# A two-layer graph network on one core: gathers behind one wait, look-ahead maxima from two tiles, sums copied a window later

## The chip, the cores and the metric

The kernel runs on 1 core of one Trainium2 chip. The metric is device time in microseconds (us) for one execution. The kernel before took 2846.57 us (median of 3 runs, 2844.92 to 2849.02).

## What is computed

The graph has N = 6250 nodes with 512 features (8 heads of 64) and E = 100000 edges, sorted by destination. Two layers follow each other, each with a normalisation in front and a residual behind:

```python
h = relu(layernorm(x))
# layer 0: attention over incoming edges
h = leaky_relu(h @ W.T + b)                       # 6250 x 512
e = leaky_relu(e_src[src] + e_dst[dst])           # per edge and head
m = segment_max(e, dst);  ex = exp(e - m[dst]);  s = segment_sum(ex, dst)
x = x + segment_sum(h[src] * (ex / s[dst] * dist), dst)
# layer 1: mean over incoming edges
h = relu(layernorm(x))
neigh = segment_sum(h[src], dst) / max(deg, 1)
y = h @ W_self.T + neigh @ W_neigh.T + bias
x = x + layernorm(y) * gamma + beta
```

## The kernel before

**Prologue** (up to about 320 us). The product `h @ W.T + b` goes to DRAM as rows of 520 values (512 features and 8 source logits), and index tables are built.

**Windows.** The edge list is cut into four streams (`NQ = 4`) that are walked side by side. A window is three tiles (`T = 3`) of 128 edges from each stream, 12 tiles in all, and there are 66 windows (`NW`; the last has one tile per stream). Streams 0 and 1 form pair p = 0, streams 2 and 3 pair p = 1. A tile is named (q, j): stream q, tile j of the window.

**Layer 0, edges** (about 320 to 1540 us). For each tile GpSimd gathers 128 rows of `h` by an indirect DMA (L719; 12 per window, in the order of `tiles`, stream by stream) into one of `NB = 4` buffers, so that `gather(k + 4)` at the end of the loop's round k refills the buffer that window k has just left. TensorE builds the one-hot of the destinations' transpose (`front_turn`, L781), multiplies it with the destinations' logits (`front_dst`, FD, L793), and adds the source logits (`soft_src`, SS, L799), which ScalarE has picked out of the gathered rows (`soft_pick`, EC, L805). So EC waits until all 12 gathers of its window have landed. VectorE finds the running maxima by three scans: `max_ahead` (NX, L824) over the next window's first two tiles backwards (`LA = 2`), `max_before` (SCF, L817) and `max_all` (SCR, L831). Two transposes (TE, TM, L843), a copy (CM), and LM, SUB, EXP, AA give the edges' weights. The weights are multiplied into the gathered rows: `message` on VectorE for tiles j = 0 and 1 (D0a, D0b, D1a, D1b, L937), and 28 pieces per window on ScalarE for most of tile 2 (H01 to H13, L956). TensorE sums the rows by destination: `add_up` (A00 to A12, L969 and L972; Apj is pair p, tile j), with `finish` (C0, C1, L980 and L981) to carry sums over from the window before. The sums of a pair fill one PSUM bank and are copied out by EV0 and EV1 (L990, L992) and stored to DRAM by `store` (L1003, SyncE's queue). A matrix product of 32-bit floats appears as two records per matmul, so an add_up is 4 records on L969 and 4 on L972.

**The order** of all this is written by hand. `ORDER` is a list of step names, gone through once per round k; `STEPS` says which window (k plus an offset) a name works on; every engine executes its own instructions in that order. "S" and "L" advance the node work (layer 0's normalisation, `slot_run`) that is mixed in.

**Layer 1, edges** (about 1590 to 2760 us). Here `gather1` (L1238) brings the 12 tiles of a window into a pool of five half-window buffers, `add_up1` (L1267) sums them, `finish1` adds the carry (L1274, two matmuls from the parts `chi` and `clo`) and copies the sums out of PSUM at once (L1277), `carry_split` (L1288, L1289) splits them for the next window's carry. Between these steps the loop at L1509 advances `slot1_run`, the dense part for 128 nodes: transposes (`turned`, L1334) with the copies `hi` and `lo` right behind them (L1335, L1336), 24 matmuls (L573), statistics and output.

Of the kernel before, what the change touches and what calls it, by code (L numbers as in the profile page):

```python
# [19 lines left out]
NQ = 4  # L20
NL = 196
ES = NL * 128
T = 3
# [21 lines left out]
def gnn_kernel(ctx, tc, x, srcp, dstp, attrp, wt0, b0, wsrc, wdst, wts, wtn, bias1, gamma1, beta1, out):  # L45
# [666 lines left out]
    def gather(k):  # L712
        GT[k] = g_ = gbuf[:, k % NB]
        tiles = [(q, j) for q in range(NQ) for j in range(njof(k))]
        if k >= NW - 3:
            tiles.sort(key=lambda t: t[1])
        for q, j in tiles:
            c = k * T + j
            G.indirect_dma_start(out=g_[:, q, j, :], out_offset=None, in_=h0_d,  # L719
                                 in_offset=bass.IndirectOffsetOnAxis(ap=idx[:, q, c:c + 1], axis=0))  # L720
# [73 lines left out]

    def soft_src(k):

        z, es = ZP[k], ES_.pop(k)
        for j in range(njof(k)):
            P.matmul(z[0:NQ * H, j * 128:j * 128 + 128], es[:, j], ident, start=False, stop=True,  # L799
                     skip_group_check=True)  # L800

    def soft_pick(k):
        nj = njof(k)
        ES_[k] = es = lp.tile([128, T, NQ * H], FT, name="es")
        A.activation(es[:, 0:nj].rearrange("p j (q h) -> p j q h", q=NQ),  # L805
                     GT[k][:, :, 0:nj, D:RW].rearrange("p q j h -> p j q h"), AF.Copy)

# [283 lines left out]
    def slot(w):  # L1091
# [140 lines left out]
    def gather1(k):  # L1232
        for p in range(2):
            GT[k, p] = g_ = g1.tile([128, 2, T, D], FT, name="g")
            for q2 in range(2):
                for j in range(njof(k)):
                    c = k * T + j
                    G.indirect_dma_start(out=g_[:, q2, j, :], out_offset=None, in_=h1_d[0:NT * 128, :],  # L1238
                                         in_offset=bass.IndirectOffsetOnAxis(ap=idx[:, 2 * p + q2, c:c + 1], axis=0))
# [19 lines left out]
    HL = {}  # L1259

    def add_up1(k, p, j):
        if j >= njof(k):
            return
        if j == 0:
            BK[p] = bank("w", 2)
        for q2 in range(2):
            P.matmul(BK[p][64 * q2:64 * q2 + 64, :], OHs[k][:, p, j, q2], GT[k, p][:, q2, j, :], start=(j == 0),  # L1267
                     stop=False, skip_group_check=True)

    def finish1(k, p):  # L1270
        w = BK.pop(p)
        if k:
            for part in HL.pop((k - 1, p)):
                P.matmul(w, CS[k][:, p], part, start=False, stop=True, skip_group_check=True)  # L1274
        if p == 0:
            WS[k] = lp.tile([128, 2, D], FT, name="ws")
        A.activation(WS[k][:, p], w, AF.Copy)  # L1277
        GT.pop((k, p))
        if p:
            OHs.pop(k)  # L1280
            CS.pop(k, None)
            WS.pop(k - 2, None)

# [30 lines left out]
    def own_run(s):  # L1314
        r, hs = SA.pop(s)
        hi, lo = parts_of(0)
        turned(hs, "t", hi, lo)
        yield
        pm = bank("m", 2)
        product(pm, hi, lo, wsh, wsl, [False])  # L1320
        P.matmul(pm, ones2, rows1, start=False, stop=True)
        yield
        OWN[s] = own = own_place(s)
# [5 lines left out]

    def turned(src, tag, hi, lo):  # L1330

        pt = bank(tag)
        for k in range(4):
            P.transpose(pt[:, k * 128:k * 128 + 128], src[:, k * 128:k * 128 + 128], ident)  # L1334
        A.activation(hi.rearrange("p k n -> p (k n)"), pt, AF.Copy)  # L1335
        V.tensor_tensor(out=lo.rearrange("p k n -> p (k n)"), in0=pt, in1=hi.rearrange("p k n -> p (k n)").bitcast(FT),  # L1336
# [25 lines left out]
    def slot1_run(s):  # L1362
        r, hs, sx, sa = SA.pop(s)
        parts = []
        for i, (src, tag) in enumerate(((hs, "t"), (sa, "z"))):
            if src is not None:
                parts.append(parts_of(i))
                turned(src, tag, *parts[-1])
            yield
        pm = bank("m", 2)  # L1370
        last = [False]
# [135 lines left out]

    last = none()
    for k in range(-1, NW - 1):  # L1509
        if k + 1 in own_at:  # L1510
            own_load(own_at[k + 1])
        early(k - 1, slot1_sums)
# [6 lines left out]
        when(k, add_up1, 0, 1)  # L1519
        step(last)  # L1520
        step(sl_)
        when(k, add_up1, 0, 2)
        step(last)
        when(k, finish1, 0)
        when(k, store, 0, acc1_d, D)
        step(last)
        step(last)
        step(sl_)
        when(k, add_up1, 1, 0)
        step(last)  # L1530
        when(k, carry_split, 0)
        step(last)
        when(k, add_up1, 1, 1)
        step(last)
        step(last)
        when(k + 1, onehot, 3)
        step(last)
        when(k, add_up1, 1, 2)
        step(last)
        when(k, finish1, 1)  # L1540
        when(k, store, 1, acc1_d, D)
        when(k, carry_split, 1)
        when(k + 1, carry_sel, FR)
        run(last)
        put_out()
        if k < NW - 2:
            step(sl_)
        early(k - 1, slot1_mean)
        run(pre)
        last = sl_  # L1550
        if k >= 0:
            when(k + 3, gather1)
    k = NW - 1
    early(k - 1, slot1_sums)
    sl_ = early(k - 2, slot1_run)
    for p in range(2):
        for j in range(T):
            add_up1(k, p, j)
        finish1(k, p)
        store(k, p, acc1_d, D)  # L1560
    for i in range(NLATE):
        late_sums(i)
    step(last)
    step(sl_)
    step(sl_)
    step(last)
    step(sl_)
# [166 lines left out]
```

## Time and profile before

| quantity | value |
|---|---|
| median of 3 runs | 2846.57 us |
| the profiled execution's own time | 2820.21 us |
| its span, first to last instruction | 2818.4 us |
| TensorE busy (PE) | 2164.9 us, 77% |
| GpSimd busy (POOL) | 1702.9 us, 60% |
| VectorE busy (DVE) | 1601.4 us, 57% |
| ScalarE busy (ACT) | 1115.8 us, 40% |
| layer 0 gathers, L719 | 784, mean 964 ns |
| layer 1 gathers, L1238 | 784, mean 982 ns |
| gathers' queue (q0), share of 16 DMA engines | 50.1% |
| mean granted TensorE clock | 0.868 |

The profiled execution ran 26 us below the median of the timed ones. Busy shares are means over stages with different limits, so a stage is read from a stretch of its own. In the timeline an entry gives the start, the length, the engine, the line, the operation, and in brackets how long the engine had been idle and what ended that; "issue" is a wait that the profile can't tell, "remote" a release without a sender in the profile.

### The profile page before, as it was taken

What the parts mean: (1) busy time and instruction counts of PE and PEld (TensorE: products, weight loads), DVE (VectorE), ACT (ScalarE), POOL (GpSimd) and SP (SyncE); (2) the same over time, 40 slices, a digit from 0 to 9 for tenths busy, and PEclk for the clock granted to TensorE, in tenths of its full rate; (3) what the DMA queues carried; (4) which work ended last, traced back from release to release, by engine and by line L of the source; (5) the groups of instructions that cost most, each with busy time, mean ns of one, the idle gap of its engine ahead of it and who ended that gap; (6) DMA issues with size and microseconds to landing.
All of it is one profiled execution on the core that took longest, in us unless ns stands there. A gap on an engine that the chain in (4) does not pass through costs nothing.

```text
span 2818.4 us, 35919 instructions
## 1 busy us (share of the span) xinstructions
PE 2164.9 (77%) x9688; PEld 1096.7 (39%) x9688; DVE 1601.4 (57%) x3323; ACT 1115.8 (40%) x3374; POOL 1702.9 (60%) x1679
## 2 busy tenths in 40 slices
PE   7993587878778778777787157797888888788775
PEld 5761244334333334333333023343433434343343
DVE  8875366566666566666667312254545445454556
ACT  5750355555555556555555201122222222222222
POOL 4665456556555556556562556666666666666662
PEclk9996688888888888889889578898999899899988
DMA  6535567777777777777776667777887787787862
GB/s 210 187 114 148 142 188 192 202 227 225 225 233 224 218 236 231 228 221 232 226 225 179 211 185 212 239 248 252 247 257 251 253 254 243 253 251 254 255 218 87
DMA packets 264720, 611.74 MB, mean 217 GB/s; under 512 B 63605, under 2 KB 74373, under 8 KB 264511
## 3 DMA queue, kind: packets, MB, share of 16 engines
q0 software_dynamic: 125440, 414.35, 50.1%
q1 hardware_dynamic: 138494, 193.97, 21.1%
q8 instruction: 80, 1.31, 0.2%
q14 instruction: 130, 1.06, 0.1%
q10 hardware_dynamic: 576, 1.05, 0.1%
HBM read 511.44 MB, written 97.76 MB: 216 GB/s over the span
## 4 chain that ended last, share of the span: by engine, by line
PE 33%; issue 21%; DVE 17%; another core or an unknown queue 11%; ACT 10%; DMA 3%; SPq 3%; POOL 1%; ACTq 0%; DVEq 0%; POOLq 0%
PE ps_w L969 9%; PE ps_w L1267 6%; ACT gbuf L956 4%; PE ps_f L573 3%; PE ps_b L573 3%; PE ps_w L980 2%; PE ps_w L1274 2%; DVE gbuf L937 2%; SPq L1003 1%; DVE hr L613 1%; POOL gbuf L719 1%; DVE clo L1289 1%; PE ps_z L793 1%; PE ps_w L573 1%
## 5 line engine op out<-in xcount | busy, mean ns | idle before, releaser
L719 POOL DMA_INDIRECT gbuf<-h_d,idx x784 | 756.1, 964 | 511.3 <-issue 251.5
L1238 POOL DMA_INDIRECT g<-h_d,idx x784 | 769.5, 982 | 395.0 <-issue 217.9
L969 PE MATMUL ps_w<-gbuf,oh 128*64 128x512 f32 x1568 | 533.0, 724 | 84.1 <-issue 62.0
L1267 PE MATMUL ps_w<-g,oh 128*64 128x512 f32 x1568 | 432.2, 652 | 104.2 <-issue 80.6
L956 ACT ACTIVATE gbuf<-gbuf,aa 128x64 f32<-128x64 f32 x1788 | 457.5, 336 | 11.2 <-DVE aa L877 5.7
L937 DVE TENSOR_TENSOR gbuf<-gbuf,ps_c 128x1024 f32<-128x1024 f32 x260 | 305.1, 1200 | 0.0
L1277 ACT ACTIVATE ws<-ps_w 128x512 f32<-128x512 f32 x132 | 78.8, 597 | 473.4 <-remote 144.6
L1288 DVE CAST chi<-ws 128x512 fp32r<-128x512 f32 x130 | 57.5, 442 | 354.0 <-issue 253.3
L1267 PEld LDWEIGHTS ps_w<-g,oh 128*64 128x64 f32 x1568 | 100.2, 146 | 275.7 <-issue 243.3
L990 ACT ACTIVATE ws<-ps_w 128x512 f32<-128x512 f32 x132 | 78.3, 593 | 260.7 <-remote 120.6
L817 DVE TENSOR_TENSOR_SCAN mf<-penb,mf,ps_z 32x384 f32<-32x384 f32 (+1 forms) x65 | 64.5, 992 | 204.6 <-ACT e L811 104.5
L608 POOL TENSOR_TENSOR pr<-hr,watt 128x1024 f32<-128x1024 f32 x47 | 113.2, 2410 | 91.3 <-DVE hr L606 75.6
L969 PEld LDWEIGHTS ps_w<-gbuf,oh 128*64 128x64 f32 x1568 | 106.9, 155 | 142.3 <-issue 106.0
L762 DVE TENSOR_TENSOR oh<-ps_c,dsr 128x768 f32<-128x768 f32 x130 | 123.4, 950 | 55.3 <-remote 26.7
L972 PEld LDWEIGHTS ps_s<-ex,oh 128*64 128x64 f32 x792 | 79.2, 161 | 181.8 <-issue 181.5
L972 PEld LDWEIGHTS ps_f<-ex,oh 128*64 128x64 f32 x776 | 73.1, 160 | 191.4 <-issue 190.5
L980 PE MATMUL ps_w<-ws,cs 128*128 128x512 f32 x228 | 138.2, 690 | 0.0
L573 PE MATMUL ps_f<-ws_whi,hi 128*128 128x512 f32 x112 | 55.6, 497 | 90.3 <-ACT hi L1335 52.2
L781 PE MATMUL ps_t<-ident,oh 128*128 128x128 f32 x392 | 75.5, 304 | 55.1 <-issue 22.2
L793 PE MATMUL ps_z<-oht,edb 128*32 128x384 f32 (+1 forms) x264 | 101.5, 509 | 19.5 <-issue 19.1
L824 DVE TENSOR_TENSOR_SCAN nx<-penb,ms,ps_z 32x256 f32<-32x256 f32 x66 | 47.5, 720 | 115.2 <-remote 94.2
L1336 DVE TENSOR_TENSOR lo<-ps_t,hi 128x512 fp32r<-128x512 f32 x55 | 37.9, 689 | 112.3 <-ACT hi L1335 67.2
(388 smaller groups left out, 3932.7 us busy)
## 6 DMA issues: line engine op xcount, KB each, us to landing
sx<-x SPq DMA_DIRECT2D x95, 256.0 KB
acc_d<-ws SPq DMA_DIRECT2D x182, 130.2 KB
acc_d<-ws SPq DMA_DIRECT2D x182, 128.0 KB
h_d<-hr SPq DMA_DIRECT2D x49, 260.0 KB
gbuf<-h_d,idx POOLq DMA_INDIRECT x784
g<-h_d,idx POOLq DMA_INDIRECT x784
sa<-acc_d SPq DMA_DIRECT2D x48, 260.5 KB
s<-acc_d SPq DMA_DIRECT2D x48, 256.0 KB
```

The source lines that it names most:

```text
L573: P.matmul(pt, a_[:, k], w_[:, k], start=not last[0], stop=stop and k == 3 and w_ is whi_ and a_ is lo)
L608: (G if t < NT - 2 else V).tensor_tensor(out=pr, in0=hr[:, None, 0:D].to_broadcast([128, 2, D]), in1=watt, op=OP.mult)
L719: G.indirect_dma_start(out=g_[:, q, j, :], out_offset=None, in_=h0_d, in_offset=bass.IndirectOffsetOnAxis(ap=idx[:, q, c:c + 1], axis=0))
L762: V.tensor_tensor(out=oh.rearrange("p a j b n -> p (a j b) n"), in0=c_iota[:, None, :].to_broadcast([128, 4 * T, M]), in1=dsr[:, k].rearra ...
L793: P.matmul(z[0:NQ * H, 0:n], ed_tile(k, p), oht[:, p, 0:n], start=(p == 0), stop=False, skip_group_check=True)
L937: eng.tensor_tensor(out=x4, in0=x4, in1=(AA if eng is V else A2)[k][:, i, q].unsqueeze(3).to_broadcast([128, 2, H, D // H]), op=OP.mult)
L956: A.activation(x_, x_, AF.Copy, scale=A2[k][:, T - 1, 2 * p + q2, h:h + 1])
L969: P.matmul(w[r, :], oh[:, p, j, q2], g_[:, 2 * p + q2, j, 0:D], start=(j == 0), stop=False, skip_group_check=True)
L972: P.matmul(sv[r, p], oh[:, p, j, q2], ex[:, j, 2 * p + q2], start=(j == 0 and p == 0), stop=False, skip_group_check=True)
L980: P.matmul(w, CS[k][:, p], c[:, p, 0:D], start=False, stop=True, skip_group_check=True)
L1238: G.indirect_dma_start(out=g_[:, q2, j, :], out_offset=None, in_=h1_d[0:NT * 128, :], in_offset=bass.IndirectOffsetOnAxis(ap=idx[:, 2 * p ...
L1267: P.matmul(BK[p][64 * q2:64 * q2 + 64, :], OHs[k][:, p, j, q2], GT[k, p][:, q2, j, :], start=(j == 0), stop=False, skip_group_check=True)
```

## The change

In layer 0:

- `gather` issues tile (3, 2) first, then the tiles j = 0, j = 1 and j = 2 of all streams (before: stream by stream). The last three windows keep their order. Tile (3, 2) is the one whose buffer is read last, by A12.
- EC and SS are split. ECa and SSa do tiles 0 and 1, at the end of the round before the one in which EC and SS stood; ECb and SSb do tile 2.
- `load_edges` loads pair 1 before pair 0.
- `ORDER` is new.

In layer 1:

- `gather1` goes tile by tile (before: stream by stream).
- `finish1` no longer copies the sums. `evac1_` does, in the next window, and issues the stores. The sums use three PSUM banks in turn instead of two.
- `turned` is split into `turn_on` (transposes) and `halves` (`hi`, `lo`), with other steps between them; the dense part of a slot ends one window later, and the loop's order is new.

```diff
     def gather(k):
...
-        if k >= NW - 3:
-            tiles.sort(key=lambda t: t[1])
+        tiles.sort(key=lambda t: (t != (NQ - 1, T - 1) or k >= NW - 3, t[1]))
...
     def load_edges(k):
...
-        for p in range(2):
+        for p in (1, 0):
...
+    def parts(k, i):
+
+        return range(0, min(LA, njof(k))) if i == 0 else range(LA, njof(k))
+
+    def soft_src(k, i):
+
+        for j in parts(k, i):
+            P.matmul(ZP[k][0:NQ * H, j * 128:j * 128 + 128], ES_[k, i][:, j - i * LA], ident, start=False, stop=True,
                      skip_group_check=True)
+        ES_.pop((k, i), None)
+
+    def soft_pick(k, i):
+        js = parts(k, i)
+        if js:
+            ES_[k, i] = es = lp.tile([128, (LA, T - LA)[i], NQ * H], FT, name=f"es{i}")
...
-        FD=(3, front_dst), EC=(2, soft_pick), SS=(2, soft_src), EZ=(2, soft_copy), SCF=(2, max_before), NX=(2, max_ahead),
+        FD=(3, front_dst), ECa=(3, soft_pick, 0), SSa=(3, soft_src, 0), ECb=(2, soft_pick, 1), SSb=(2, soft_src, 1), EZ=(2, soft_copy), SCF=(2, max_before), NX=(2, max_ahead),
...
-    H01 S CS H10 FT1 D0a S TE EC SS A00 D1a H11 D0b S H02 EV1 RESC H03 D0c L S A01 AT0 OH S A10 FT1c H12 D1b A02 S NX S SCR RS
-    FL FDf FX RH S C0 AT0c FT0 AT1 H13 EV0 S A11 TM EZ SCF S CM LM PF S SUB F9a F9b S A12 EXP S C1 AA AT1c FD S FT0c
+    FT1 S H10 D0a TE S H01 L CS D1a A00 D0b ECb NX SCR EV1 RESC A01 H13 D0c A10 S H03 SSb S H02 S FT1c H12 OH H11 AT0 S
+    TM FL FDf FX CM D1b A02 LM S RS SUB EZ S RH C0 FT0 AT0c EV0 AT1 SCF S EXP PF S A11 AA S F9a A12 F9b C1 AT1c FD ECa
+    S SSa S FT0c
...
     def gather1(k):
...
-            for q2 in range(2):
-                for j in range(njof(k)):
+            for j in range(njof(k)):
+                for q2 in range(2):
...
+    def bank_s():
+
+        s_[0] = (s_[0] + 1) % 3
+        return bank("s") if s_[0] == 0 else bank("w", 2)
...
     def finish1(k, p):
...
-        if p == 0:
-            WS[k] = lp.tile([128, 2, D], FT, name="ws")
-        A.activation(WS[k][:, p], w, AF.Copy)
+        BK[k, p] = w
...
+    def evac1_(k, p):
+        if p == 0:
+            WS[k] = lp.tile([128, 2, D], FT, name="ws")
+        A.activation(WS[k][:, p], BK.pop((k, p)), AF.Copy)
+        store(k, p, acc1_d, D)
...
     def slot1_run(s):
...
+                pts.append(turn_on(src, tag))
             yield
+        for i, pt in enumerate(pts):
+            parts.append(parts_of(i))
+            halves(pt, *parts[-1])
+        yield
...
-    last = none()
+    last, ends = none(), none()
     for k in range(-1, NW - 1):
...
+        when(k - 1, evac1_, 0)
+        early(k - 2, slot1_mean)
+        step(sl_)
         when(k, add_up1, 0, 0)
+        step(ends)
+        when(k - 1, carry_split, 0)
...
+        when(k, finish1, 0)
         step(sl_)
+        run(ends)
+        put_out()
+        when(k - 1, evac1_, 1)
+        early(k - 1, slot1_sums)
+        when(k, add_up1, 1, 0)
+        when(k - 1, carry_split, 1)
...
-        last = sl_
+        last, ends = sl_, last
```

More of the change, by code (lines that the diff above doesn't have):

```diff
@@ L793, in front_dst @@
             P.matmul(z[0:NQ * H, 0:n], ed_tile(k, p), oht[:, p, 0:n], start=(p == 0), stop=False, skip_group_check=True)
-    def soft_src(k):
-        z, es = ZP[k], ES_.pop(k)
-        for j in range(njof(k)):
-            P.matmul(z[0:NQ * H, j * 128:j * 128 + 128], es[:, j], ident, start=False, stop=True,
-                     skip_group_check=True)
[L802 to L806, printed above, removed]
+    def parts(k, i):
[3 more added lines that the diff above has]
+            P.matmul(ZP[k][0:NQ * H, j * 128:j * 128 + 128], ES_[k, i][:, j - i * LA], ident, start=False, stop=True,
+                     skip_group_check=True)
+        ES_.pop((k, i), None)
[3 more added lines that the diff above has]
+            ES_[k, i] = es = lp.tile([128, (LA, T - LA)[i], NQ * H], FT, name=f"es{i}")
+            A.activation(es[:, 0:len(js)].rearrange("p j (q h) -> p j q h", q=NQ),
+                         GT[k][:, :, js[0]:js[-1] + 1, D:RW].rearrange("p q j h -> p j q h"), AF.Copy)
     def soft_copy(k):
@@ L1234, in gather1 @@
             GT[k, p] = g_ = g1.tile([128, 2, T, D], FT, name="g")
-            for q2 in range(2):
-                for j in range(njof(k)):
+            for j in range(njof(k)):
+                for q2 in range(2):
                     c = k * T + j
@@ L1259, in gnn_kernel @@
     HL = {}
+    s_ = [0]
+    def bank_s():
+        s_[0] = (s_[0] + 1) % 3
+        return bank("s") if s_[0] == 0 else bank("w", 2)
     def add_up1(k, p, j):
@@ L1264, in add_up1 @@
         if j == 0:
-            BK[p] = bank("w", 2)
+            BK[p] = bank_s()
         for q2 in range(2):
@@ L1281, in finish1 @@
             CS.pop(k, None)
+    def evac1_(k, p):
[3 more added lines that the diff above has]
+        store(k, p, acc1_d, D)
+        if p:
             WS.pop(k - 2, None)
@@ L1315, in own_run @@
         r, hs = SA.pop(s)
+        pt = turn_on(hs, "t")
+        yield
+        yield
         hi, lo = parts_of(0)
-        turned(hs, "t", hi, lo)
+        halves(pt, hi, lo)
         yield
@@ L1321, in own_run @@
         P.matmul(pm, ones2, rows1, start=False, stop=True)
+        yield
         yield
@@ L1328, in parts_of, with turn_on @@
         return [lp.tile([128, 4, 128], FR, name=f"{n_}{i}", bufs=1) for n_ in ("hi", "lo")]
-    def turned(src, tag, hi, lo):
+    def turn_on(src, tag):
         pt = bank(tag)
@@ L1334, in turned, with halves @@
             P.transpose(pt[:, k * 128:k * 128 + 128], src[:, k * 128:k * 128 + 128], ident)
+        return pt
+    def halves(pt, hi, lo):
         A.activation(hi.rearrange("p k n -> p (k n)"), pt, AF.Copy)
@@ L1363, in slot1_run @@
         r, hs, sx, sa = SA.pop(s)
-        parts = []
-        for i, (src, tag) in enumerate(((hs, "t"), (sa, "z"))):
+        pts, parts = [], []
+        for src, tag in ((hs, "t"), (sa, "z")):
             if src is not None:
-                parts.append(parts_of(i))
-                turned(src, tag, *parts[-1])
+                pts.append(turn_on(src, tag))
             yield
+        for i, pt in enumerate(pts):
+            parts.append(parts_of(i))
+            halves(pt, *parts[-1])
+        yield
         pm = bank("m", 2)
@@ L1511, in gnn_kernel @@
             own_load(own_at[k + 1])
-        early(k - 1, slot1_sums)
         early(k, slot1_load)
@@ L1515, in gnn_kernel @@
         pre = early(k, slot1_pre)
+        when(k - 1, evac1_, 0)
+        early(k - 2, slot1_mean)
+        step(sl_)
         when(k, add_up1, 0, 0)
+        step(ends)
+        when(k - 1, carry_split, 0)
         step(last)
-        step(sl_)
-        when(k, add_up1, 0, 1)
-        step(last)
[L1521 to L1549, printed above, removed]
-        last = sl_
+        step(ends)
+        when(k, add_up1, 0, 1)
+        step(ends)
+        when(k + 1, onehot, 3)
+        step(ends)
+        step(last)
+        step(ends)
+        when(k, add_up1, 0, 2)
+        step(ends)
+        when(k, finish1, 0)
+        step(sl_)
+        run(ends)
[4 more added lines that the diff above has]
+        when(k - 1, carry_split, 1)
+        when(k + 1, carry_sel, FR)
+        when(k, add_up1, 1, 1)
+        when(k, add_up1, 1, 2)
+        step(sl_)
+        run(pre)
+        when(k, finish1, 1)
+        step(last)
+        last, ends = sl_, last
         if k >= 0:
@@ L1553, in gnn_kernel @@
     k = NW - 1
+    sl_ = early(k - 2, slot1_run)
+    evac1_(k - 1, 0)
+    carry_split(k - 1, 0)
+    evac1_(k - 1, 1)
     early(k - 1, slot1_sums)
-    sl_ = early(k - 2, slot1_run)
+    early(k - 2, slot1_mean)
+    carry_split(k - 1, 1)
     for p in range(2):
@@ L1559, in gnn_kernel @@
         finish1(k, p)
-        store(k, p, acc1_d, D)
+        evac1_(k, p)
     for i in range(NLATE):
         late_sums(i)
+    step(sl_)
     step(last)
     step(sl_)
+    step(last)
     step(sl_)
+    run(ends)
+    put_out()
     step(last)
```

## The prediction

> **What bounds the kernel now.** I read the slices of the page first: from 320 to 1540 us (layer 0's edges) and from 1590 to 2760 us (layer 1's) no engine is full, PE stands at 7 to 8 tenths, the DMA engines at 7. So something repeats with a hole in it. The timeline of GpSimd shows layer 0's period, 12 gathers (columns: start, length, engine, line, operation; in brackets the idle time before and its end):
>
> ```profile
> 705.43 0.94 POOL L719 DMA_INDIRECT gbuf<-h_d,idx  x1 [0.30 <-issue]
> 708.95 0.95 POOL L719 DMA_INDIRECT gbuf<-h_d,idx  x1 [2.57 <-remote]
> 710.20 1.01 POOL L719 DMA_INDIRECT gbuf<-h_d,idx  x1 [0.30 <-issue]
> 713.06 0.94 POOL L719 DMA_INDIRECT gbuf<-h_d,idx  x1 [1.86 <-ACT gbuf L956]
> ...
> 724.75 0.95 POOL L719 DMA_INDIRECT gbuf<-h_d,idx  x1 [0.30 <-issue]
> 728.04 0.94 POOL L719 DMA_INDIRECT gbuf<-h_d,idx  x1 [2.34 <-remote]
> ```
>
> One round runs from 708.95 to 728.04. Inside it there are two holes: after two gathers (the third waits for the old window's tile 2, stream 0, read last by H0x and A02), and at the end (the next first gather waits for A00 of the next window). Over the three rounds from 708.95: first to third gather 4.0 us, third to twelfth 11.55, twelfth to the next first 3.5; 19.05 together. L831, once a window, gives 18.9 over 400 to 1400 us. Free gathers follow each other by 0.95 + 0.30, 1.27 with the few long ones.
>
> What is the last hole? The same stretch on PE, then on ScalarE:
>
> ```profile
> 716.95 1.12 PE L980 MATMUL ps_w<-ws,cs 128*128 128x512 f32 x2
> ...
> 722.38 1.06 PE L969 MATMUL ps_w<-gbuf,oh 128*64 128x512 f32 x4
> 724.48 0.17 PE L972 MATMUL ps_f<-ex,oh 128*64 128x9 f32 x1 [1.05 <-issue]
> 725.90 0.17 PE L972 MATMUL ps_f<-ex,oh 128*64 128x9 f32 x1 [1.25 <-issue]
> 727.47 0.30 PE L972 MATMUL ps_f<-ex,oh 128*64 128x9 f32 x2 [1.40 <-issue]
> ```
> ```profile
> 714.10 0.60 ACT L990 ACTIVATE ws<-ps_w 128x512 f32<-128x512 f32 x1 [1.95 <-issue]
> ...
> 725.20 0.60 ACT L990 ACTIVATE ws<-ps_w 128x512 f32<-128x512 f32 x1 [2.73 <-issue]
> 727.50 0.19 ACT L992 ACTIVATE ws<-ps_s 128x18 f32<-128x18 f32 x1 [1.70 <-remote]
> ```
>
> C0's L980 ended at 714.06 and its copy EV0 started 0.04 us later. C1's L980 ended at 718.07, and its copy EV1 started at 725.20, its second part at 727.50. So while gathers flow, PE's completions reach the others late, and they all arrive when the gathers drain, here at 727.5: VectorE's NX starts at 727.76 after 1.46 us of "remote", GpSimd at 728.04. PE itself ran on for 32 matmuls from C1, then went in single steps of about 1.4 us. Completions were prompt until 7.0 us into the round (TM ended 715.95, CM began 715.98), and C1's, 9.1 us in, were not. By this reading a wait for PE costs nothing if it can be met by a matmul that is done by the drain, and costs its distance from the drain otherwise. The clock has the same period:
>
> ```profile
> core 0: us, PE busy (x) PEld busy (x) DVE busy (x) ACT busy (x) POOL busy (x), PEclk, DMA share, GB/s
> ...
> 708.00:713.00 5.00, 4.58 (x18) 2.31 (x19) 1.94 (x4) 3.71 (x16) 1.96 (x2) 0.50 0.47 121
> ...
> 717.00:724.00 7.00, 6.21 (x34) 2.86 (x33) 6.78 (x15) 5.44 (x20) 5.48 (x6) 1.00 0.95 313
> 724.00:728.00 4.00, 0.87 (x6) 0.66 (x7) 2.54 (x5) 1.10 (x4) 1.39 (x2) 0.89 0.71 218
> ```
>
> After the hole PE runs at clock 0.50: an L969 group of four takes 2.02 us at 727.54 against 1.06 at 722.38.
>
> **Layer 0, part by part.** The new order of gathers begins with tile (3, 2), whose reader A12 is the window's last; the other eleven find their buffers free. The inner hole goes: a round is 11 x 1.27 = 14.0, plus the 3.5 of landing and release that the rows show, plus X, the time from the drain until A12 is done and seen. 17.5 + X stands against 19.1, so **X = 1.6 us is the point of no gain**.
>
> X by bounds. Below: 0, A12 done by the drain. Above: in the trace of before A12's matmuls ended at about 716.8, 8.4 us after the drain at 708.4. Between them I count matmuls in the new order, 78 a window as now. The work from C1 on, at the warm clock: C1 with its L981 1.18 us, FD 1.41, SSa 0.56 (four of six of L799's 0.84), FT1 0.47, TE 0.37 and its 0.23 of idle time, A00 and A01 1.0 each; 6.2 us and 34 matmuls to A10. PE's first 4.6 busy us after a drain run at clock 0.50 (the row of 708 to 713) and so lose 2.3. From the drain to the last prompt completion it has 0.5 us (727.5 to 728.04), X, and 7.0 to 9.1 us, less 2.3. Then 32 matmuls run ahead and some four step, so 42 must fit before.
> With 7.0: say 10 matmuls of A11 and A12 are left at the drain, 1.25 us warm, 2.5 cold, X = 2.5 - 0.5 = 2.0; what PE has is 0.5 + 2.0 + 7.0 - 2.3 = 7.2 warm us, 5.95 after the rest, which is 32 matmuls; 10 + 32 = 42 fits. With 9.1: nothing left, X = 0; 0.5 + 9.1 - 2.3 = 7.3 us is all 34 and nine of A10 and SSb; 43 fits. So X lies at 0 to 2.0 in this count, and I take the middle, **1.0**, as no row says where between 7.0 and 9.1 the hold begins. 18.5 against 19.1 is -0.6 us, over the 59 windows that the new order holds for (4 to 62): **-35 us**. The ends: X = 0, -1.6 x 59 = -94; X = 8.4, +6.8 x 59 = +401.
>
> On the wait that is added: behind it in GpSimd's queue stand the eleven other gathers of the round and nothing else. Who needs them first is ECa at the next round's end: nine gathers, 9 x 1.27 + 3.5 = 15 us after the start, before the 17.5 of a round; ECb comes later. If that cover went, PE would stand at SSa by the difference.
>
> Small terms. The split of EC adds one activation; the nearest row is L805 with 0.27 us, L992 with 0.19: ScalarE is busy 113 of 200 us at 700 to 900, so it hides; uncovered, 0.27 x 59 = 16. NX and SCR (0.73 and 1.01) now start from SSa, six steps earlier than their use: they leave the stretch after the drain, where NX waited 1.46 to 2.00 us; that is part of X being small. TM, however, stands before A02 now and is probably seen only at the drain, so CM, LM, SUB, EXP, AA (0.33 + 0.36 + 0.26 + 0.28 + 0.53, and EZ and SCF between) run after it, some 3.5 us, beside C1, FD, SSa, FT1, TE (4.0); if they fall out longer A00 waits for D0a. `load_edges` swaps two loads on SyncE's queue whose first user comes a round later: nothing. Without that cover FD would wait for one load.
>
> [...]
>
> **Layer 1, part by part.** The lines of 1900 to 2500 us:
>
> ```profile
> L1238 POOL DMA_INDIRECT g<-h_d,idx x410 | 404.1, 986 | 196.7 <-issue 113.7 <-remote 32.8 <-PE ps_w L1267 17.4
> L573 PE MATMUL ps_b<-ws_whi,hi 128*128 128x512 f32 x60 | 28.7, 479 | 32.0 <-ACT hi L1335 32.0
> ```
>
> 410 gathers are 34.2 windows of 17.56 us. Busy 404.1 and spacing 113.7 make 15.15 a window; the other 83.0, **2.43 us a window**, is GpSimd waiting for buffers, so for PE. PE waits for `hi` 32.0, and 6.5 more in the second product: 1.1 us a window. The split of `turned` puts steps between the transposes and the copies, and the copies before the product: this wait should go. The late copy of the sums (0.60, then 0.44 and 0.69 for the parts) must be done before the next `finish1`, which stands behind three add_up1 of 1.08 us: 1.73 against 3.2, hidden; the third bank keeps add_up1 from waiting for it. What is late next is the completion of add_up1 itself. I take half of the 1.1, as a wait that ends also lets PE run into the next one: -0.6 x 62 windows = **-37 us**. The ends: the whole hole, -2.43 x 62 = -150; the copy chain uncovered, +1.7 x 62 = +105. Gathers by tile: the data are used two windows later, nothing. On SyncE stores now go before the sums' loads, which wait for them; L1038 waits 4.5 us for such loads in 34 windows now, 0.13 each, and the slot has one window more.
>
> **Sum.** -35 - 37 = -72. The profiled execution took 2820.21 us (span 2818.4), 26 below the median of 2846.57; I take the difference over to the median: 2846.6 - 72 = **2775 us**.
>
> **Rivals.**
> - *One layer alone gains* (about 2810): X is 1.6 and layer 1 gives its 37, or the wait for `hi` only moves and layer 0 gives its 35. For it: both terms are middles between bounds.
> - *Slower: A12 is late.* Place: the wait of the first gather. If all of A11 and A12 is left at the drain, 16 matmuls, the cold 2.02 us for each make X = 4.0 - 0.5 = 3.5, and (17.5 + 3.5 - 19.1) x 59 = +112, with layer 1's -37 that is 2922; a rest of two matmuls less gives X = 3.0 and 2892. It decides from X = 1.6 in layer 0, from 2.2 for the sum. For it: one wait on the last reader leaves no slack, TM's chain after the drain; against it: the count above, if the hold begins after 7.0 us.
> - *No difference* (2847): transfers limit it, and the holes were hidden. Against: the DMA share is 0.77 over 700 to 900 us; 19.1/18.5 makes it 0.80.
> - *Much faster* (2580): completions come promptly in the new phase; a round is 12 x 1.27 = 15.2, -3.9 x 59 = -230, with -37. Against: each of 33 rounds that I looked at had the hold until the drain.
>
> **Chances.** Forecast (2725 to 2800) 0.40, one layer 0.13, much faster 0.08: faster 0.61. No difference 0.05. Slower 0.34. About 0.2% is what a measurement tells from no change. Leaving out the 0.08 below and some 0.12 of the slow end gives 2685 (both layers near their good ends: X = 0 and -67 in layer 1) to 2900 (X = 3.1).
>
> **What would show it.** Right: rounds of 12 gathers without the inner hole, 3.5 + 1.0 before the next; L831 every 18.5 us; NX without "remote"; L573 without the wait for `hi`, L1238's idle rest below 2.43. Wrong: a hole above 5.1 us ahead of the first gather, A11 and A12 cold after the drain; in layer 1 the wait passing to L1274 (`chi`) or to the bank.

## The result, and the profile after

| | before | after | ratio, 95% interval |
|---|---|---|---|
| the runs shown | 2846.27 us (4 runs) | **3015.86 us** (4 runs) | 1.0576 [1.0539, 1.0613] |
| profiled execution, span | 2818.4 us | 3010.2 us | |
| first gather of layer 1 starts at | 1580.5 us | 1757.9 us | |
| first to last gather of layer 1 | 1152.2 us | 1169.2 us | |
| layer 0, one window (windows 15 to 55) | 19.28 us | 22.50 us | |
| mean granted TensorE clock | 0.868 | 0.831 | |

The ratio is the one on record for all executions; the quotient of the two medians is 1.0596, inside its interval.

The change made the kernel 170 us slower; the forecast was 72 us faster, with a range that ended at 2900. Nearly all of it is layer 0. Between the two profiled executions, whose spans differ by 192 us because that of before ran 26 us below its median, 177 us lie ahead of the first gather of layer 1. The 17 us behind it are hardly more than the 15 us by which profiles with the old layer 1 differ among themselves (first to last gather 1152 us here, 1167 us in before_new_gather_order_4, a run below).

One thing is needed to read the experiments: on the chips used for them the kernel before took 2816 to 2853 us in some sessions and 2394 to 2397 us in others, so every run is compared with the kernel before in its own session, and I call the two kinds **held** (as in the runs shown) and **free** by what their traces show.

The flow of GpSimd in the kernel after, at the end of one round and the start of the next (line numbers moved: L718 is the gather):

```profile
722.62 0.95 POOL L718 DMA_INDIRECT gbuf<-h_d,idx  x1 [0.30 <-issue]
723.87 0.95 POOL L718 DMA_INDIRECT gbuf<-h_d,idx  x1 [0.30 <-issue]
731.92 0.94 POOL L718 DMA_INDIRECT gbuf<-h_d,idx  x1 [7.10 <-issue]
733.16 0.95 POOL L718 DMA_INDIRECT gbuf<-h_d,idx  x1 [0.30 <-issue]
```

The hole after two gathers is gone, as the forecast had it: twelve gathers take 14.1 us from the first start to the last. But the hole ahead of the first gather is 8.0 us here, 8.4 in the mean of the rounds from 600 to 1300 us, where 3.5 + 1.0 was forecast. What PE does up to that wait's end (A02 with its L976, C0, FT0, then A11 and A12):

```profile
716.62 1.08 PE L973 MATMUL ps_w<-gbuf,oh 128*64 128x512 f32 x4
717.52 0.24 PE L976 MATMUL ps_f<-ex,oh 128*64 128x9 f32 x4
717.69 0.70 PE L984 MATMUL ps_w<-ws,cs 128*128 128x512 f32 x1
718.64 0.59 PE L984 MATMUL ps_w<-ws,cs 128*128 128x512 f32 x1 [0.25 <-issue]
720.09 0.25 PE L985 MATMUL ps_f<-ws,cs 128*128 128x9 f32 x1 [0.86 <-issue]
722.25 0.17 PE L985 MATMUL ps_f<-ws,cs 128*128 128x9 f32 x1 [1.91 <-issue]
722.95 0.37 PE L780 MATMUL ps_t<-ident,oh 128*128 128x128 f32 x1 [0.53 <-issue]
725.04 0.37 PE L780 MATMUL ps_t<-ident,oh 128*128 128x128 f32 x1 [1.72 <-issue]
726.55 0.37 PE L780 MATMUL ps_t<-ident,oh 128*128 128x128 f32 x1 [1.14 <-issue]
727.26 1.99 PE L973 MATMUL ps_w<-gbuf,oh 128*64 128x512 f32 x4 [0.34 <-issue]
729.01 0.37 PE L976 MATMUL ps_f<-ex,oh 128*64 128x9 f32 x4
729.19 1.99 PE L973 MATMUL ps_w<-gbuf,oh 128*64 128x512 f32 x4
```

PE falls into single steps at 718.64, only 8.7 us after the round's first gather (709.91), at C0. Six matmuls take until the drain; all of A11 and A12 is left, and runs at half speed: 1.99 us for a group of four against 1.08 at 716.62. The next first gather starts at 731.92, just after A12. The same stretch by slices (columns as in the prediction's table):

```profile
715.00:718.60 3.60, 3.39 (x27) 1.64 (x23) 3.53 (x6) 1.11 (x5) 2.84 (x3) 1.00 0.83 235
718.60:727.20 8.60, 2.12 (x6) 0.87 (x5) 0.21 (x1) 0.00 (x0) 4.73 (x5) 0.73 0.74 214
727.20:732.00 4.80, 4.74 (x17) 2.12 (x18) 3.95 (x15) 4.09 (x16) 0.08 (x1) 0.50 0.37 116
```

In the middle stretch PE is busy 2.12 of 8.6 us and VectorE and ScalarE hardly at all. VectorE shows that A11 and A12 did not wait for their data: D1b, the last message, ended at 718.81 (ScalarE's last piece of tile 2 at 716.12), and VectorE then stands until LM (L859), which follows ScalarE's CM (727.55). CM's source TM was done on PE at 716.69 and was seen only at the drain.

```profile
717.62 1.19 DVE L941 TENSOR_TENSOR gbuf<-gbuf,ps_c 128x1024 f32<-128x1024 f32 x1
727.91 0.36 DVE L859 SCALAR_TENSOR_TENSOR et<-ps_b,et 128x192 f32<-128x192 f32 x1 [9.10 <-ACT et L852]
```

### The profile page after: what moved, and what is told of

It is laid out like the page before. It is cut to its first block, busy times and chain, and to the rows that moved or that the text cites. A ratio compares the mean times of both kernels' runs of the same rounds, so it can differ in the third digit from the quotient of the medians.

```text
span 3010.2 us, 36047 instructions
## 1 busy us (share of the span) xinstructions
PE 2236.1 (74%) x9688; PEld 1106.6 (37%) x9688; DVE 1608.4 (53%) x3323; ACT 1110.7 (37%) x3439; POOL 1716.8 (57%) x1679
## 4 chain that ended last, share of the span: by engine, by line
PE 30%; issue 10%; POOL 4%; DVE 3%; DMA 2%; ACT 1%; SPq 0%; another core or an unknown queue 0%; DVEq 0%; POOLq 0%; ACTq 0%
PE ps_w L1279 8%; PE ps_f L573 5%; PE ps_b L573 4%; POOL g L1243 4%; PE ps_s L1279 4%; PE ps_w L973 2%; PE ps_w L1286 2%; DMA g<-h_d,idx 1%; PE ps_s L1286 1%; PE ps_w L984 1%; PE ps_z L1355 1%; PE ps_t L1355 1%; DVE sx L1044 0%; PE ps_t L780 0%; DVE gbuf L941 0%
## 5 line engine op out<-in xcount | busy, mean ns | idle before, releaser
L718 POOL DMA_INDIRECT gbuf<-h_d,idx x784 | 766.3, 977 | 673.7 <-issue 287.4
L973 PE MATMUL ps_w<-gbuf,oh 128*64 128x512 f32 x1568 | 510.9, 732 | 31.9 <-issue 23.0
L1279 PE MATMUL ps_w<-g,oh 128*64 128x512 f32 x1048 | 316.8, 662 | 92.0 <-issue 85.1
L859 DVE SCALAR_TENSOR_TENSOR et<-ps_b,et 128x192 f32<-128x192 f32 x66 | 23.4, 354 | 504.8 <-ACT et L852 481.3
L852 ACT ACTIVATE et<-ps_b 128x192 f32<-128x192 f32 x66 | 21.6, 327 | 598.8 <-remote 510.3
L984 PE MATMUL ps_w<-ws,cs 128*128 128x512 f32 x228 | 166.7, 791 | 81.0 <-issue 80.9
L1279 PE MATMUL ps_s<-g,oh 128*64 128x512 f32 x520 | 161.7, 668 | 23.6 <-issue 21.5
L780 PE MATMUL ps_t<-ident,oh 128*128 128x128 f32 x392 | 96.0, 343 | 102.4 <-issue 90.1
L1279 PEld LDWEIGHTS ps_w<-g,oh 128*64 128x64 f32 x1048 | 73.0, 145 | 229.3 <-issue 217.7
L976 PEld LDWEIGHTS ps_s<-ex,oh 128*64 128x64 f32 x792 | 71.7, 159 | 167.0 <-issue 166.7
L976 PEld LDWEIGHTS ps_f<-ex,oh 128*64 128x64 f32 x776 | 69.0, 159 | 171.3 <-issue 171.1
L1361 DVE TENSOR_TENSOR lo<-ps_z,hi 128x512 fp32r<-128x512 f32 x48 | 33.1, 689 | 151.6 <-issue 106.8
L792 PE MATMUL ps_z<-oht,edb 128*32 128x384 f32 (+1 forms) x264 | 104.3, 519 | 10.2 <-DVE mf L821 4.9
L780 PEld LDWEIGHTS ps_t<-ident,oh 128*128 128x128 f32 x392 | 55.4, 173 | 137.2 <-issue 135.7
```

The costliest lines, as they stand in the source:

```text
L780: P.transpose(pt[:, j * 128:j * 128 + 128], OHs[k][:, p, j].rearrange("e b n -> e (b n)"), ident)
L973: P.matmul(w[r, :], oh[:, p, j, q2], g_[:, 2 * p + q2, j, 0:D], start=(j == 0), stop=False, skip_group_check=True)
L976: P.matmul(sv[r, p], oh[:, p, j, q2], ex[:, j, 2 * p + q2], start=(j == 0 and p == 0), stop=False, skip_group_check=True)
L984: P.matmul(w, CS[k][:, p], c[:, p, 0:D], start=False, stop=True, skip_group_check=True)
```

## The experiments

Two theories. **H (horizon)**: in a held session PE gets a fixed number of matmuls, some 50, from the start of an unbroken flow of gathers, whatever comes first in the flow. The change removed the break after two gathers, so the flow begins 4 us earlier in PE's work, and what lies beyond the horizon, A12 among it, is done after the drain. **O (order)**: the loss comes from the new order of steps, TM ahead of A02, so that CM to AA and the messages run after the drain.

All results (median us; ratio on record to the kernel before in the same session, which differs from the quotient of the medians by up to 0.2%). after_pause_6, before_new_gather_order_4 and before_spaced have two executions each, the others 4 to 12:

| run | session, before | this | ratio, 95% interval |
|---|---|---|---|
| l0_only | free, 2397.03 | 2403.52 | 1.0032 [1.0015, 1.0048] |
| l1_only | free, 2397.03 | 2403.40 | 1.0026 [1.0012, 1.0039] |
| before_new_gather_order | free, 2397.03 | 2432.59 | 1.0160 [1.0136, 1.0185] |
| after_stream_order | free, 2397.03 | 2407.12 | 1.0042 [1.0025, 1.0059] |
| after_again (gathers by tile) | free, 2396.68 | 2404.06 | 1.0034 [1.0020, 1.0049] |
| after_pause_2 | free, 2396.68 | 2599.65 | 1.0869 [1.0839, 1.0899] |
| after_here | **held**, 2850.51 | 3021.93 | 1.0610 [1.0583, 1.0637] |
| before_loaded | **held**, 2850.51 | 2848.19 | 1.0000 [0.9973, 1.0027] |
| before_new_gather_order_2 | free, 2396.01 | 2424.87 | 1.0119 [1.0089, 1.0149] |
| after_stream_order_2 | free, 2396.01 | 2403.25 | 1.0024 [1.0009, 1.0040] |
| after_pause_2_2 | free, 2396.01 | 2599.95 | 1.0846 [1.0807, 1.0886] |
| before_spaced | free, 2396.01 | 2551.56 | 1.0646 [1.0605, 1.0688] |
| before_new_gather_order_3 | free, 2394.01 | 2424.68 | 1.0130 [1.0102, 1.0157] |
| after_pause_6 | **held**, 2816.21 | 2862.70 | 1.0174 [1.0116, 1.0232] |
| after_stream_order_3 | **held**, 2819.16 | 2831.26 | 1.0036 [0.9991, 1.0081] |
| before_new_gather_order_4 | **held**, 2852.91 | 3086.28 | 1.0818 [1.0770, 1.0866] |
| l1_only_2 | **held**, 2836.85 | 2844.98 | 1.0012 [0.9990, 1.0034] |
| after_by_tile_2 | **held**, 2845.67 | 2786.66 | 0.9803 [0.9744, 0.9861] |

### The two layers apart: l0_only, l1_only

The file of before up to `gather1` joined with the rest of after (l1_only), and the other way round (l0_only).

> Layer 0 of the kernel after, layer 1 of the kernel before. If the parts add up, as the two traces suggest (first layer-1 gather 177 us later, layer 1's edges 17 us longer than in the profiled execution of before, which was itself 26 us under its median), the time is 2995 to 3025. If layer 1 carries more of the loss than that, it is under 2980.

> Layer 0 of the kernel before, layer 1 of the kernel after. By the traces 2840 to 2865: no gain, the wait for hi gone and the same time lost in steps of PE while gathers flow. The prediction's step for layer 1 (-37) would give 2810.

Both fell on a free session, and both parts cost 0.3%: the expected times belong to held sessions, so they say nothing for or against them. What a free session looks like, layer 0 of the kernel after, from 699 to 740 us: each of its 32 gathers, more than two rounds, follows the one before after 0.30 or 0.31 us, as these five do:

```profile
709.06 0.95 POOL L718 DMA_INDIRECT gbuf<-h_d,idx  x1 [0.30 <-issue]
710.31 0.95 POOL L718 DMA_INDIRECT gbuf<-h_d,idx  x1 [0.30 <-issue]
711.56 0.94 POOL L718 DMA_INDIRECT gbuf<-h_d,idx  x1 [0.30 <-DVE mr L835]
712.81 1.27 POOL L718 DMA_INDIRECT gbuf<-h_d,idx  x1 [0.30 <-issue]
714.38 0.94 POOL L718 DMA_INDIRECT gbuf<-h_d,idx  x1 [0.30 <-issue]
```

Gathers run back to back in both layers, 15.3 to 15.5 us a window in each of them, and GpSimd sets the time. The waits of PE over 400 to 1400 us (line, what it waited for, us in all, times, longest), first the kernel after in the runs shown, then l0_only:

```profile
PE ps_w L984 <- issue: 62.2, 59, 2.0
PE ps_t L780 <- issue: 54.3, 55, 2.0
PE ps_f L985 <- issue: 35.7, 29, 2.0
PE ps_f L976 <- issue: 29.6, 23, 2.7
```
```profile
PE ps_w L973 <- ACT ws L994: 57.2, 30, 6.1
...
PE ps_z L801 <- ACT es L809: 31.4, 22, 3.0
...
PE ps_w L973 <- issue: 1.4, 1, 1.4
```

The waits for "issue", which are the single steps, are there in the one kind of session (262 us over all lines in the kernel after) and not in the other (1.4 us).

Later the part of layer 1 was run in a held session:

> Layer 0 of before, layer 1 of after, once more for a session of the slow kind (before 2810 to 2850). The traces of that kind show a layer-1 window of 17.55 and 17.74 us with the old layer 1 and of 17.57, 17.59, 17.84 and 17.96 with the new one, so 0 to +0.5%. The prediction's step (-37 us) would give -1.3%. In a session in which before takes about 2400: +0.3% as measured.

It came out at 1.0012 [0.9990, 1.0034]: layer 1's part neither gains nor loses. The forecast's -37 us would be 0.987.

### The order of the gathers alone

The kernel before with one edit; nothing else of the change.

```diff
-        if k >= NW - 3:
-            tiles.sort(key=lambda t: t[1])
+        tiles.sort(key=lambda t: (t != (NQ - 1, T - 1) or k >= NW - 3, t[1]))
```

> The kernel before with one edit: gather brings tile (3, 2) first, then by tile. The order of the steps stays that of before. Theory H (horizon): in an unbroken flow of gathers PE gets only some 52 matmuls done and its completions are unseen until the drain; 78 matmuls lie between A12 and A12 whatever the order, so the same 17 or so are left, cold, and a round takes about 22.4 us: 2846 + 59 x 3.4 = 3046, or 3020 to 3060. Theory O (order): the loss comes from the new order of steps, TM ahead of A02, whose completion is seen only at the drain so that CM to AA and the messages run late; with the old order the round loses its inner hole and nothing else, 2750 to 2850.

> The kernel before with the new order of gathers alone, again, meant for a chip on which the kernel before takes about 2850 us. There: theory H (horizon: some 50 matmuls in an unbroken flow, whatever the order) 3020 to 3060; theory O (the new order of steps makes the loss) 2750 to 2860. On a chip where before takes about 2400 us: 2432 as measured.

> The kernel before with the new order of gathers alone, once more, meant for a chip on which the kernel before takes about 2850 us. There: theory H (horizon: some 50 matmuls in an unbroken flow, whatever the order of steps) 3020 to 3060; theory O (the new order of steps makes the loss) 2750 to 2860. On a chip where before takes about 2400 us: 2425 to 2433 as measured.

> The kernel before with the new order of gathers alone, once more for a session of the slow kind (before 2810 to 2850). There: theory H 59 x 3.1 to 3.4 us more than before, 2990 to 3050; if the new gather order is only bad together with the new order of steps, 2800 to 2900. In a session in which before takes about 2400: 2425 to 2433 as measured.

The first three fell on free sessions, 1.2 to 1.6% slower. The fourth fell on a held one: 3086 us, 233 more than before, above H's range and far from O's. In its trace a round ends like this:

```profile
737.85 0.95 POOL L718 DMA_INDIRECT gbuf<-h_d,idx  x1 [0.31 <-issue]
747.59 0.95 POOL L718 DMA_INDIRECT gbuf<-h_d,idx  x1 [8.79 <-PE ps_s L971]
```

The wait for A12 is 9.7 us from start to start, a window 23.56 us. So one line of the change makes a loss larger than the whole change, with the old order of steps. O falls.

### The order of the gathers undone

The kernel after with that line set back; the new order of steps, the split of EC and SS, and layer 1 stay.

> The kernel after with the gathers of layer 0 in the order of before (stream by stream); the new order of steps stays. Theory H: the hole after two gathers comes back, the unbroken flow starts 4 us later, PE gets its 18 to 20 matmuls more, a round takes about 19 us: 2840 to 2900, layer 1's part included. Theory O: the loss stays, 2980 to 3030.

> The kernel after with the gathers of layer 0 stream by stream, again, meant for a chip on which the kernel before takes about 2850 us. There: theory H 2840 to 2900 (the hole after two gathers comes back, PE gets the 18 to 20 matmuls); theory O 2980 to 3030. On a chip where before takes about 2400 us: 2407 as measured.

> The kernel after with layer 0's gathers stream by stream, once more for a session of the slow kind (before 2810 to 2850). There: theory H 2840 to 2900, a round of about 19 us, with the hole after two gathers back; theory O 2980 to 3030. In a session in which before takes about 2400: 2403 to 2407 as measured twice.

In the held session 1.0036 [0.9991, 1.0081], 9 us under H's range: with the old order of gathers the loss is gone. This is the same finding from the other side. The window is 19.44 us, the break after two gathers is back, and PE's waits for "issue" over 400 to 1400 us are 147 us, as in the kernel before (148).

### A pause inside the flow

The kernel after with one instruction more, behind the second gather of a window (after_pause_2: i == 1) or behind the sixth (after_pause_6: i == 5). It reads one column of the tile just gathered, so it waits until that has landed.

```diff
+            if i == 5 and NB <= k < NW - 3:
+                G.tensor_tensor(out=junk[:, 0:1], in0=g_[:, q, j, 0:1], in1=g_[:, q, j, 0:1], op=OP.add)
```

> The kernel after with one GpSimd instruction of one element per partition behind the second gather of a window, which waits until that gather has landed: the hole inside the flow comes back, at a cost of about 3 us of GpSimd's time a window. Where the kernel before takes about 2846 us: theory H says PE gets 18 to 20 matmuls more ahead of the drain and the hole before the first gather shrinks by 4 us or more, so an added pause makes the kernel faster: a round of 19.5 us for 22.4, 2840 to 2900. Theory O says the pause changes nothing or adds up to 3 us a window, 3010 to 3190. Where the kernel before takes about 2400 us and GpSimd sets the period, the pause costs its full length: 59 x 3 = 175 us on about 2410.

> The kernel after with a pause of GpSimd behind the second gather of a window, until that has landed; again, meant for a chip on which the kernel before takes about 2850 us. There: theory H says that a pause of 3 us makes the kernel after faster, as completions and instructions come through in it: 2840 to 2930 against 3020. Theory O: 3010 to 3190. On a chip where before takes about 2400 us: 2600 as measured.

> The kernel after with the pause of GpSimd in the middle of the flow, behind the sixth gather. Where the kernel before takes about 2850 us: theory H says two flows of six gathers (7.6 us each) never reach the horizon of some 8.5 us, PE is not starved, and the round is 12 x 1.27 + 3 + 3.5 at most, 19 to 21 us, 2840 to 2940 against 3020; theory O 3010 to 3190. Where before takes about 2400 us the pause costs its length as behind the second gather, 2590 to 2610.

In free sessions the pause behind the second gather costs its length, 8.5 to 8.7%. In a held session the pause behind the sixth makes the kernel after **faster**: 1.0174 against before, where the kernel after is at 1.0576 and 1.0610. GpSimd in that run:

```profile
712.35 0.19 POOL L722 TENSOR_TENSOR junk<-gbuf 128x1 f32<-128x1 f32 x1 [3.48 <-DMA gbuf<-h_d,idx]
712.99 0.96 POOL L719 DMA_INDIRECT gbuf<-h_d,idx  x1 [0.45 <-issue]
...
726.87 0.94 POOL L719 DMA_INDIRECT gbuf<-h_d,idx  x1 [0.30 <-issue]
731.43 0.51 POOL L722 TENSOR_TENSOR junk<-gbuf 128x1 f32<-128x1 f32 x1 [3.62 <-DMA gbuf<-h_d,idx]
732.08 0.97 POOL L719 DMA_INDIRECT gbuf<-h_d,idx  x1
733.35 1.38 POOL L719 DMA_INDIRECT gbuf<-h_d,idx  x1 [0.30 <-issue]
```

A break of 5.2 us from start to start is added to each window, and the window falls from 22.5 to 19.74 us: the break lets A12 be done and seen, so that the next window's first gathers follow the flow with little or no hole (1.81 us from start to start in the mean, where it was 8.4). The kernel after lost its time for want of a break, which is what H says, and the time is in H's range. But H's reason was two flows of six gathers, and that is not what happened: between the two pauses shown twelve gathers follow each other, six of one window and six of the next, and of the 69 flows that begin between 400 and 1400 us (a flow ends where two gathers start more than 1.9 us apart) 35 have twelve gathers and 28 have six. So twelve gathers without a break do not cost by themselves; it matters whether the matmul that the next gather waits for is done by the drain. The break behind the second gather has no run in a held session.

### By tile, without a leader

```diff
-        tiles.sort(key=lambda t: (t != (NQ - 1, T - 1) or k >= NW - 3, t[1]))
+        tiles.sort(key=lambda t: t[1])
```

The kernel after, but tile (3, 2) is not pulled ahead. The waits lie spread over the twelve gathers (label after_again in the free session).

> The kernel after with its gathers by tile, but tile (3, 2) in its natural place, last but none ahead of the others: the wait is spread over the tiles (A00 first, then A10, A01, A11, A02, A12). Where the kernel before takes about 2846 us: theory H says the waits for A11 and later readers cannot be met while gathers flow, the flow stops for a drain in the middle and PE gets its horizon twice, a round of 19 to 20.5 us, 2850 to 2930; theory O (order) says the loss of the kernel after stays, 2980 to 3030. Where the kernel before takes about 2400 us (no completions held, gathers back to back): 2400 to 2425, as the other parts alone.

> The kernel after with tile (3, 2) in its natural place, once more for a session of the slow kind (before 2810 to 2850). Theory H: its first gather waits only for A00, but the later readers' completions are not seen in the flow, so it breaks by itself in the middle and drains there; 2830 to 2930, perhaps a little under the kernel before if the break is short. If a wait for the last reader is bad wherever it stands in the order, 2980 to 3030. In a session in which before takes about 2400: 2404 as measured.

In held sessions this is the **fastest of the kernels run: 2786.66 us, 0.9803 [0.9744, 0.9861]** of before, and under H's range; in the free one it is 0.3% slower than before, like the other parts. GpSimd in the held run:

```profile
712.19 0.95 POOL L718 DMA_INDIRECT gbuf<-h_d,idx  x1 [0.30 <-issue]
715.20 0.95 POOL L718 DMA_INDIRECT gbuf<-h_d,idx  x1 [2.06 <-PE ps_b L847]
...
721.45 0.95 POOL L718 DMA_INDIRECT gbuf<-h_d,idx  x1 [0.30 <-issue]
724.35 0.94 POOL L718 DMA_INDIRECT gbuf<-h_d,idx  x1 [1.96 <-PE ps_f L985]
```

The flow breaks by itself every six gathers, for 1.8 to 2.1 us of idle time. The two holes of a window are of one length and lie evenly, where the kernel before has 1.5 to 1.9 and 2.3 to 2.8 us of idle time in its two, and a window takes 18.44 us for 19.28. PE still goes in single steps: its waits for "issue" over 400 to 1400 us come to 151 us, as many as in the kernel before (148; the kernel after has 262). The two longest groups:

```profile
PE ps_w L973 <- issue: 45.5, 57, 2.2
PE ps_b L847 <- issue: 21.6, 28, 2.0
```

In 62 of the 99 flows of six that begin between 400 and 1400 us PE waits for "issue" for 0.5 us or more (from 2 us behind the flow's start on, up to the next flow), the first time after 26 matmuls in the mean; in after_pause_6, whose breaks are longer, it does so in 3 of 28. So H's number of some 50 does not hold for short flows with short breaks, and the gain is not that PE runs freely. What differs from the kernel after is one line, and with it the 8.4 us ahead of the first gather. It is not the wait for the last reader by itself that costs, but one wait whose matmuls are not done when the flow ahead of it has drained.

### Again the kernel after, and a load on the transfers

after_here is the kernel after unchanged. before_loaded is the kernel before with a copy that nothing uses:

```diff
+        if 4 <= k < NW - 6:
+            A.dma_start(ld_d[0:256, :], x[0:256, :])
```

> The kernel after, unchanged, on a chip of the experiments. Where the kernel before takes about 2400 us, GpSimd issues gathers back to back in both layers (15.3 to 15.5 us a window), so that neither the one wait nor the order of steps can cost a round: the two parts alone gave +0.3% each, so 2405 to 2420. If the one wait on A12 is bad by itself, 2450 or more. Where the kernel before takes about 2846 us: 3016 as shown.

> The kernel before with a copy of 512 KB from DRAM to DRAM in each layer-0 window, issued from ScalarE, whose result nothing uses. It asks whether it is the load of the transfers that holds PE's completions back. Theory C (contention): with the DMA share pushed from 0.89 towards 1, PE shows single steps put down to issue and completions that arrive at the drain, as in the profile of before; layer 0's window goes from 15.4 us to 19 or more. Theory N (not the load): the windows grow only by what the gathers' transfers take longer, 15.4 to 17, and PE shows no idle time put down to issue.

A held session: the loss is there again, 1.0610. The copies (512 KB in each of 56 windows) change nothing, 1.0000 [0.9973, 1.0027]; the window is 19.40 us where the profile of before had 19.28. The DMA share over 700 to 900 us is 0.79 where it was 0.77, so the added load is small and this run alone says little about C. More is said by a profile of the free kind: in l0_only the DMA share of the same stretch is 0.89, above that of every held profile (0.77 before, 0.64 after, at most 0.79), and PE shows no single steps. A high mean load of the transfers is therefore not enough to bring the hold about; whether more of it would do so in a free session was not tried.

### Gathers further apart

```diff
+            if NB <= k < NW - 3:
+                G.tensor_tensor(out=junk[:, 0:64], in0=ident[:, 0:64], in1=ident[:, 0:64], op=OP.add)
```

> The kernel before with a GpSimd addition of 64 elements per partition behind each layer-0 gather, which waits for nothing: gathers follow each other more slowly, by an estimated 0.2 to 0.4 us more than the 1.25. Where the kernel before takes about 2850 us: if the hold comes from gathers issued too close together, PE's single steps vanish and a round takes 12 x 1.5 + 1 = 18 to 19 us, 2780 to 2850; if it comes with any unbroken flow, the flow is only longer, 11 x 0.25 = 3 us more a round, 2950 to 3030. Where it takes about 2400 us: GpSimd sets the period, 15.4 goes to about 18.4, 2560 to 2600.

A free session: GpSimd's period goes to 17.95 us a window (four gathers from 700 us on start 1.44 to 1.61 us apart, with 1.25 for free ones), 2552 us, a little under what was expected. Whether a slower flow would be held as well stays open.

## Why the prediction was wrong, point by point

- **The bound.** That completions wait for the drain in a flow of gathers, and that the wait of the first gather is paid by the distance of its reader from the drain, was right: TM, done on PE at 716.69, was taken up by CM on ScalarE at 727.55, and the pause (after_pause_6), an edit that does nothing else, took the hole ahead of the first gather of a window from 8.4 to 1.81 us from start to start in the mean.
- **The step that failed** is the count for X: "From the drain to the last prompt completion it has 0.5 us (727.5 to 728.04), X, and 7.0 to 9.1 us". The 7.0 and 9.1 us were read in the kernel before and counted from the round's first gather. But there the flow is broken after two gathers and begins at the third, 4.1 us later; from there the same rows say 2.9 us (TM) and 5.0 us (C1). I took away the break and kept the time that the break had given. In matmuls: before, PE's first single step comes 54 matmuls after the third gather (mean over 600 to 1300 us, up to the first wait for "issue" of 0.5 us or more; 22 to 64 in single rounds); after, it comes 53 matmuls after the first (24 to 65), and 54 in the round of 709.91. Six steps and the 16 matmuls of A11 and A12 make up the 78, with C1's two ahead of the first gather.
- **What the right count gives.** 78 - 54 - 6 = 18 matmuls beyond the drain, 0.25 us each at the cold clock (the prediction's 2.02 us for eight; eight take 1.93 us from 727.26 to 729.19 above), is 4.5 us, less 0.5: X = 4.0. The prediction's own working, with 5.0 and 2.9 us in place of 9.1 and 7.0, closes at the same X = 4.0 (18 matmuls left and 24 fitting before make 42) and at X = 6.0 (26 and 16). The measured hole of 8.4 less the 3.5 is 4.9, where the sum had 1.0. At 4.0 a round is 21.5, +2.4 x 59 = +142, so about 2990 without a gain in layer 1.
- **The rival "A12 is late"** had the place, the mechanism and the 16 matmuls; it was put at 2922 with 0.34 for all slower outcomes. Its price was 1.4 us a window too low in X, and layer 1 did not give its 37.
- **The inner hole** went as forecast, and was counted as a gain of 2.7 us a window. It was worth more than it cost: between the first and the third gather of a window PE did 18 matmuls (mean of windows 20 to 54), and these now fall behind the start of the flow.
- **The wait behind which eleven gathers stand**: ECa did not wait for them to any length (5.9 us for L809 over 45 windows). Right.
- **TM's chain after the drain**: seen as foreseen (VectorE idle 9.10 us for it), and hidden beside A11 and A12. The rest of the change, the new order of steps among it, did not cost: with the same gathers the ratio is 1.0576 to 1.0610 with it and 1.0818 without it.
- **The clock.** The count took from the row of 708 to 713 us that PE starts cold after the drain. The kernel after shows the same: behind the stepped stretch, from 727.2 to 732.0 us, PE is busy 4.74 of 4.8 us at a clock of 0.50. In the stretch itself, with PE busy 2.12 of 8.6 us and 1.91 us as its longest wait for "issue", the mean clock is 0.73, and it is 1.00 in the 3.6 us ahead of it. PE's waits for "issue" from 400 to 1400 us are at most 2.7 us in either kernel. What sets the granted clock was not shown.
- **Layer 1.** The wait for `hi` went, as forecast, and PE's time went elsewhere. Lines of 2080 to 2680 us of the kernel after:

```profile
L1243 POOL DMA_INDIRECT g<-h_d,idx x400 | 395.7, 989 | 204.9 <-issue 110.0 <-PE ps_w L1279 35.4 <-remote 32.6
...
L573 PE MATMUL ps_f<-wn_whi,hi 128*128 128x512 f32 x56 | 26.0, 464 | 15.7 <-issue 15.5
...
L573 PE MATMUL ps_b<-ws_whi,hi 128*128 128x512 f32 x56 | 23.6, 422 | 0.1
```

  L573 no longer waits for `hi` (0.1 us where it was 32.0), but three lines of the product with `wn` into `ps_f` now stand 46 us for "issue", in single steps, where they stood 5.8 and the line of `ws` 27.8. GpSimd's waits beyond its spacing are (204.9 - 110.0) / 33.3 = 2.85 us a window where they were 2.43, and its two breaks of 2.3 us, one in the window's middle and one at its edge, became 3.5 and 1.5. What the prediction took for small is the wait for the loads of the sums: ScalarE's is 90.4 us here (L1385) where it was 4.3 (L1360); PE hardly waits for it (0.1 us at L1355). The term of the sum was -37; measured 0 (1.0012 [0.9990, 1.0034]). "A wait that ends lets PE run into the next one" was the reason to take half; it took the whole.
- **The range** left out what lay above 2900 as 0.12. It was built from the count, and the count had one source for its times; the bound of +401 was in the text and should have weighed more, as nothing but that count stood against it.

## What to carry to other kernels

A hole in a timeline may be what lets another engine move (here 18 matmuls in the inner hole): before taking it away, count from its end, not from the round's start, what is done in it and because of it. A time read off a trace ("prompt until 7 us") belongs to the event that starts its clock, so look for the event that the change leaves in place. One wait ahead of a long row of transfers makes the row unbroken, and if its matmuls are not done when the row has drained, the row stands still for them, here for 8.4 us a window from start to start; the same waits spread over the row can be cheaper, as they were here by 8% of the time of before in held sessions (1.0576 and 1.0610 against 0.9803).

## What the runs showed of the hardware

- In held sessions PE gets about 50 matmuls in the mean from the start of an unbroken flow of ten or twelve gathers (54 in the kernel before, 53 in the kernel after, 49 in before_new_gather_order_4, up to the first wait for "issue" of 0.5 us or more, over 600 to 1300 us), then single steps of 1 to 2 us until the gathers have drained. Whether a count of matmuls or a time is behind it no run separates (10.2, 8.6 and 9.1 us in the same three), and in the flows of six of after_by_tile_2 the steps come earlier, after 26 matmuls in the mean.
- Held and free sessions differ by 19% for the same kernel (2847 against 2397), and a chip that was held in one session was free in a later one (chip 10: before 2850.51, later 2394.01). Nothing in the kernels makes the difference, and the prologue shows none: the first gather starts at 240.3 us in the profile of before and at 237.8 to 243.2 us in free sessions. What holds the completions, and why not always, stays open; a load of 512 KB a window, which takes the DMA share from 0.77 to 0.79, does not deepen it, and a free profile has no hold at a share of 0.89.
- What a change is worth depends on this: a pause behind the second gather makes the kernel after some 8% slower in a free session (2600 us against 2404 for its form by tile), and one behind the sixth took some 4% off it in held sessions (1.0174 against 1.0576 and 1.0610); the gathers' order is +1.2 to +1.6% in the one, +8.2% in the other. Here no version was faster in a free session, and one, by tile without a leader, was faster in a held one.
